# The eighth product with B of a selective scan, formed on GpSimd in ten of sixteen blocks

## The chip, the cores and the metric

The kernel runs on one core of a Trainium2 chip. The metric is device time in microseconds (us). A NeuronCore has five engines that run side by side: TensorE (PE, matrix products), VectorE (DVE), ScalarE (ACT), GpSimd (POOL) and SyncE (SP, here it starts most of the DMAs). Each works through its own queue in order; where one needs another's result, it waits on a semaphore.

## The reference, cut to what matters

Two residual layers of mixer and feed-forward network over `x` (2 x 512 tokens of 512). The change lies in the first mixer, a Mamba block with 1024 channels and 16 states per channel:

```python
def step(state, inp):
    dt_t, B_t, C_t, u_t = inp
    dA = jnp.exp(dt_t[..., None] * A)
    state = state * dA + (dt_t * u_t)[..., None] * B_t[:, None, :]
    y = jnp.einsum('bdn,bn->bd', state, C_t)
    return (state, y)
...
_, ys = jax.lax.scan(step, init, xs)
y = ys.transpose(1, 0, 2) + x * D
y = y * jax.nn.silu(gate)
return y @ W_out.T
```

Behind it come a feed-forward layer with 4-bit weights, an attention over heads within each token, and a second feed-forward layer with experts; each is normalised before and after.

## The kernel before

**Tiling of the scan.** The channels are cut into 8 chunks of 128, one per partition; with two batches that makes 16 blocks (`order`, batch 0 first). A block's 16 states are taken two at a time (`NG = 2`), so a block has 8 steps, and the scan 128. In this text block k is the k-th of the 16 and step g the group of two states within it; step number `s` is 8k + g. Time (512) lies along the free dimension, so that one instruction on 128x1024 elements does two states over all of time.

**What a step does.** On ACT, `exps` (L1002) makes the decay factors `da` = exp(dt A) for the two states, in one of two PSUM buffers that alternate from step to step; it does so for step s + 2, after the scan of step s. On DVE, `times_B` (L1018) forms `bx` = du x B in SBUF, where `du` = dt x u lies in PSUM and holds for the whole block (ACT copies dt there, L1010 in `new_du`; DVE multiplies by u, L1016, at step 0), and `scan` (L1022) runs the recurrence in place, `state = da * state + bx`. On POOL, `times_C` (L1028) multiplies the states by C in place. On PE, `sums` (L1041) adds the two states to the block's `y` in PSUM by products with the identity; the first of a block also adds D x u (L1036). At step 2 of the next block, `fin` (L1047) multiplies `y` by the gate on DVE.

**What sets the order.** The instructions of every engine run in the order in which the program traces them (`pin` ties each to the one before it on its engine, for PE, ACT, DVE and POOL). The main loop (from L1063) writes one pass per step s: the sums of step s - 2 and as much other PE work as a budget of 3.5 us per step allows (`STEP`), then a `tick`, the B product of step s + 1, a second `tick`, the scan of s, the factors of s + 2, the C product of s. A `tick` advances a counter by one and resumes those jobs (generators started by `spawn`) whose time has come; each yields the number of ticks until its next piece. Through them runs everything beside the scan: gates (`silu_of`, three ACT operations L682 to L684 and a product on POOL, L687), the second batch's convolution, the output product of the first batch with its norms (L119, L125, L127, L134, L855, L868), and the first batch's feed-forward layer `ffn0` (PE L947, DVE L935). `pool_turn` keeps such jobs from putting more than one product on POOL in the same step; `pool_at[0]` holds the step whose turn is taken.

**Buffers.** `bx` tiles come from a pool `bxp` of six buffers of 4 KB per partition in turn; one is free again once PE has summed it. `du`, `y` and each `da` have their own place in PSUM. The B and C rows of a batch are spread over all partitions (`states`, L540), one SBUF tile for each step; those of the second batch are loaded by SP during block 7, each after the last use of the tile by the first batch. Behind them on SP's queue come the loads of the output weights `wo` (L862).

**After the scan** PE goes on with what is left of `ffn0`, then the output product of the second batch (L1124), the down product of the first batch's feed-forward layer (L1146), and so on to the end.

Of the kernel before, what the change touches and what calls it, by code (L numbers as in the profile page):

```python
# [9 lines left out]
F32 = mybir.dt.float32  # L10
# [8 lines left out]
P = 128  # L19
B = 2  # L20
S = 512
# [13 lines left out]
NG = 2  # L35
NGI = N_ST // NG
# [20 lines left out]
def tile_sandwich(  # L57
# [5 lines left out]
    nc = tc.nc  # L63

    def pool(scope, name, bufs=1, space=None):
        kw = {"space": space} if space is not None else {"reuse_waits": "tile"}
        return scope.enter_context(tc.tile_pool(name=name, bufs=bufs, **kw))
# [108 lines left out]
    scans, now = [], [0]  # L176
    pool_at = [-9]
# [223 lines left out]
    def pin():  # L401

        seen = nc.cur_bb.bb.instructions
        for ins in seen[behind.get("n", 0) :]:
            if ins.engine not in ORDERED:
                continue
            prev = behind.get(ins.engine)
            if prev is not None:
                tc.add_manual_dep(
                    ins, prev.name,  # L410
                    mybir.DependencyInfo(mybir.DependencyClass.NoSync, mybir.DependencyReason.DATA),
                    reason="order of tracing",
                )
            behind[ins.engine] = ins
        behind["n"] = len(seen)
# [6 lines left out]
    with ExitStack() as mamba:  # L422
# [33 lines left out]
        Bbs = [[None] * NGI for _ in range(B)]  # L456
        Cbs = [[None] * NGI for _ in range(B)]
        st = {}
# [21 lines left out]
        def diag(k):  # L480

            c = k % NCH
            t_ = dgp.tile([P, P], F32, tag="dg", name=f"dg{k}")
            nc.scalar.activation(t_, ident, AF.Copy, scale=ch[:, c, KCONV + 1 : KCONV + 2])
            st["diag", k] = t_
# [49 lines left out]
        def states(b, gi):  # L535

            for lst, lo, nm in ((Bbs[b], 0, "B"), (Cbs[b], R_C - R_B, "C")):
                t_ = bcp.tile([P, NG, S], F32, tag=f"{nm}{gi}", name=f"{nm}{b}_{gi}")
                n0 = lo + gi * NG
                ins = nc.sync.dma_start(  # L540
                    out=t_, in_=scr[b][n0 : n0 + NG, :].partition_broadcast(P)
                )
                lst[gi] = t_
            return ins

        def dt_in(b, c):
            ps = mbank(f"pv{b}_{c}")
            nc.tensor.matmul(ps, wdt[:, ts(c, P)], dtT[b], start=True, stop=True)
            return ps
# [98 lines left out]
            return g1p.tile([P, cols], dt, tag=f"g1{i}", name=name)  # L648

        with ExitStack() as p2:  # L650
            bxp = pool(p2, "bx", 6)
            ps_y = pool(p2, "p2y", 1, PSUM)
            ps_du = pool(p2, "p2du", 1, PSUM)
            ps_da1 = pool(p2, "p2da1", 1, PSUM)
# [13 lines left out]
            def spawn(gen, lag=0):  # L668
                jobs.append([now[0] + lag, gen])

            def tick():
                now[0] += 1
                for job in list(jobs):
                    if job[0] <= now[0]:
                        try:
                            job[0] = now[0] + next(job[1])
                        except StopIteration:
                            jobs.remove(job)
# [13 lines left out]
            def bank_free():  # L692
                return len(turns) < 2 or turns[-2][1] is not None
# [299 lines left out]
            order = [(b, c) for b in range(B) for c in range(NCH)]  # L993
            NS = len(order) * NGI
            bxs = {}

            def exps(s):
                k, gi = divmod(s, NGI)
                b, c = order[k]
                for i in range(NG):  # L1000
                    n = gi * NG + i
                    nc.scalar.activation(  # L1002
                        das[s % 2][:, i, 1:], st["dt", b, c][:, 1:], AF.Exp, scale=A[:, c, n : n + 1]
                    )

            def new_du(k):

                b, c = order[k]
                du = st["du"] = ps_du.tile([P, S], F32, tag="du", name=f"du{b}_{c}")
                nc.scalar.copy(du, st["dt", b, c])  # L1010

            def times_B(s):
                k, gi = divmod(s, NGI)
                b, c = order[k]
                if gi == 0:
                    nc.vector.tensor_mul(st["du"], u[b][c], st["du"])  # L1016
                bx = bxs[s] = bxp.tile([P, NG, S], F32, tag="bx", name=f"bx{b}_{c}_{gi}")
                nc.vector.tensor_mul(bx, st["du"].unsqueeze(1).to_broadcast([P, NG, S]), Bbs[b][gi])  # L1018

            def scan(s):  # L1020
                flat = bxs[s].rearrange("p n t -> p (n t)")
                nc.vector.tensor_tensor_scan(  # L1022
                    flat, das[s % 2].rearrange("p n t -> p (n t)"), flat, 0.0, ALU.mult, ALU.add
                )

            def times_C(s):
                b, c = order[s // NGI]
                nc.gpsimd.tensor_mul(bxs[s], bxs[s], Cbs[b][s % NGI])  # L1028

            def sums(s):  # L1030
                k, gi = divmod(s, NGI)
                b, c = order[k]
                cost = NG * MM
                if gi == 0:
                    y = st["y"] = ps_y.tile([P, S], F32, tag="y", name=f"py{b}_{c}")
                    nc.tensor.matmul(y, st["diag", k], u[b][c], start=True, stop=False)  # L1036
                    cost += MM
                bx = bxs.pop(s)
                for i in range(NG):
                    n = gi * NG + i  # L1040
                    nc.tensor.matmul(st["y"], ident, bx[:, i, :], start=False, stop=(n == N_ST - 1))  # L1041
                return cost

            def fin(k):

                b, c = order[k]
                nc.vector.tensor_mul(g[b][c], g[b][c], st["y"])  # L1047
                st[f"fin{k}"] = now[0]

            def dt_job(k, ps):  # L1050
                dt_out(*order[k], ps)
                release(f"pv{k}")
                yield 1
# [5 lines left out]
            exps(0)  # L1059
            exps(1)  # L1060
            times_B(0)
            free, dt_due = 0.0, None
            for s in range(NS + 3):  # L1063
                k, gi = divmod(s, NGI)
                free = min(free, MM) + STEP
                if gi == 1 and k + 1 < len(order):
                    dt_due = k + 1
                if gi == 2 and k:
                    fin(k - 1)
                for part in ((1, 0) if gi == 2 else (0, 1)):  # L1070
                    if part == 0:
                        if 0 <= s - 2 < NS:
                            free -= sums(s - 2)
                    else:
                        while free > 0 and s < NS:
                            if dt_due and bank_free():
                                turns.append([f"pv{dt_due}", None])
                                spawn(dt_job(dt_due, dt_in(*order[dt_due])), 2)
                                free -= MM
                                dt_due = None  # L1080
                            cost = next(pe, None)
                            if cost is None:
                                break
                            free -= cost
                tick()
                if gi == 4 and k + 1 < len(order):
                    diag(k + 1)
                if 0 < s < NS - 1:
                    times_B(s + 1)
                    if gi == NGI - 2 and k + 1 < len(order):  # L1090
                        new_du(k + 1)
                tick()
                if s < NS:
                    scan(s)
                    if s == 0:
                        times_B(1)
                    if s + 2 < NS:
                        exps(s + 2)
                    times_C(s)
                    if order[k] == (0, NCH - 1):  # L1100
                        states(1, gi)
                pin()
# [6 lines left out]
        with ExitStack() as p3:  # L1109
# [9 lines left out]
            for j in range(NCH // 2):  # L1119
                w = wo_pair(1, 0, j)  # L1120
                for e in range(2):
                    c = 2 * j + e
# [305 lines left out]
```

## Time and profile before

| | us |
|---|---|
| median of 3 runs | 965.91 (965.67 to 966.76) |
| the profiled execution | 963.47 |
| its span, first to last instruction | 961.7 |
| DVE busy over the span | 676.8 |
| PE busy | 869.3 |
| POOL busy | 464.0 |
| ACT busy | 420.7 |
| first scan starts, last scan ends | 74.2, 571.1 |

The profile is of one execution, with every instruction's start and duration. "Busy" is the time in which an engine had an instruction under way; PE's matrix products overlap at their ends, so a busy PE isn't PE at its peak: in the scan's busiest stretches products of 128x512 follow each other every 0.43 us while each is shown as 0.59 us long. Idle time of an engine is put down to the instruction that ended it, shown after an arrow. More than half of the span is the scan, and the kernel's time is the end of the chain that runs through it and the layers behind it.

### The profile page before, as it was taken

Reading aid. Unit: us, or ns where it says so; the run is one execution under the profiler, and the core shown is the slowest. Engines: PE = TensorE matmul, PEld = TensorE weight load, DVE = VectorE, ACT = ScalarE, POOL = GpSimd, SP = SyncE. Lnnn points to the kernel's source line nnn. Section 1 sums busy time; section 2 is a strip of 40 time slices with the busy share of each in tenths; the row PEclk is TensorE's granted clock in tenths of the full one; section 3 lists DMA queues with packets and bytes.
Section 4 is the critical chain, followed back from the end, with each engine's and each line's share of the span. In section 5 each row is a group of like instructions: output and inputs, shape, how many; then the busy total and the mean of one; then the engine's idle time right before and its main releaser. Section 6 shows DMA issues by size and latency. Waiting matters only on the chain.

```text
span 961.7 us, 7188 instructions
## 1 busy us (share of the span) xinstructions
PE 869.3 (90%) x2216; PEld 391.1 (41%) x2216; DVE 676.8 (70%) x783; ACT 420.7 (44%) x631; POOL 464.0 (48%) x335
## 2 busy tenths in 40 slices
PE   6967979878999799769999999998999998999994
PEld 3533433323543344324443434444544444445441
DVE  5959999999999989999989977334510024525225
ACT  4245775656667646565656421124320013412122
POOL 6656796776877757777767664330000000001002
PEclk9988999999999999999999999999999999999998
DMA  6349011100003833300110114336122231100101
GB/s 200 143 159 394 22 37 37 37 29 30 22 26 134 295 128 131 110 0 5 40 44 22 29 40 147 133 127 212 55 62 74 63 100 44 65 12 22 55 0 44
DMA packets 43816, 80.08 MB, mean 83 GB/s; under 512 B 7774, under 2 KB 20937, under 8 KB 43778
## 3 DMA queue, kind: packets, MB, share of 16 engines
q1 hardware_dynamic: 41506, 73.64, 22.6%
q0 software_dynamic: 1984, 5.47, 1.5%
q10 hardware_dynamic: 288, 0.52, 0.1%
q8 instruction: 17, 0.28, 0.1%
q14 instruction: 21, 0.17, 0.1%
HBM read 68.37 MB, written 11.24 MB: 83 GB/s over the span
## 4 chain that ended last, share of the span: by engine, by line
PE 49%; DVE 27%; issue 10%; POOL 5%; DMA 3%; ACT 1%; SPq 0%; DVEq 0%; POOLq 0%; ACTq 0%
DVE bx L1022 10%; PE py L1041 8%; DVE bx L1018 8%; PE pd L1356 6%; PE pup L1293 5%; PE fo L1146 4%; PE fu L367 3%; PE fo L1209 3%; PE fg L367 3%; PE fu L947 3%; POOL bx L1028 3%; PE po L1124 3%; PE fg L947 2%; DMA B<-scr 2%; DVE u L475 2%
## 5 line engine op out<-in xcount | busy, mean ns | idle before, releaser
L1028 POOL TENSOR_TENSOR bx<-bx,C 128x1024 f32<-128x1024 f32 x128 | 302.1, 2360 | 134.3 <-DVE bx L1022 118.1
L1022 DVE TENSOR_TENSOR_SCAN bx<-da,bx 128x1024 f32<-128x1024 f32 x128 | 291.4, 2277 | 0.1
L1041 PE MATMUL py<-bx,ident 128*128 128x512 f32 x512 | 249.0, 617 | 38.3 <-POOL bx L1028 38.2
L1002 ACT ACTIVATE da<-dt,A 128x511 f32<-128x511 f32 x256 | 176.6, 691 | 163.2 <-DVE bx L1022 158.5
L1041 PEld LDWEIGHTS py<-bx,ident 128*128 128x128 f32 x512 | 96.6, 195 | 171.9 <-issue 96.9
L1018 DVE TENSOR_TENSOR bx<-du,B 128x1024 f32<-128x1024 f32 x128 | 154.0, 1204 | 9.5 <-DMA wgu_d<-w_gu 6.2
L1222 DVE TENSOR_TENSOR it<-it,fu 128x512 f32<-128x512 f32 (+1 forms) x11 | 7.6, 687 | 73.9 <-PE fu L367 73.9
L1293 PE MATMUL pup<-hT_l,wup 128*128 128x512 f32 x128 | 57.2, 602 | 0.0
L709 PE MATMUL pg<-xT,w_g 128*128 128x512 f32 x120 | 56.3, 597 | 0.0
L1356 PE MATMUL pd<-wdn,hid 128*128 128x512 f32 x128 | 56.3, 601 | 0.0
L381 POOL TENSOR_TENSOR sd<-ve,half 128x4 f16<-128x4 f16 x2 | 2.1, 1044 | 110.5 <-DVE ve L379 110.5
L127 POOL TENSOR_TENSOR rs_lo<-ve_lo,mhalf 128x1 f32<-128x1 f32 x8 | 5.5, 683 | 78.3 <-DVE ve_lo L125 78.3
L947 PE MATMUL fu<-hT_f,wu 128*128 128x512 f32 (+1 forms) x88 | 41.5, 593 | 0.7 <-ACT dt L553 0.7
L947 PE MATMUL fg<-hT_f,wg 128*128 128x512 f32 (+1 forms) x88 | 41.6, 595 | 0.0
L367 PE MATMUL fg<-hT_f,wg 128*128 128x512 f32 (+1 forms) x88 | 40.2, 593 | 0.7 <-ACT hT_f L171 0.7
L367 PE MATMUL fu<-hT_f,wu 128*128 128x512 f32 (+1 forms) x88 | 40.7, 603 | 0.0
L475 DVE SCALAR_TENSOR_TENSOR u<-px,ch,u 128x511 f32<-128x511 f32 (+2 forms) x48 | 35.8, 746 | 6.1 <-ACT u L468 4.9
L1209 PE MATMUL fo<-wd,it 128*128 128x512 f32 (+1 forms) x88 | 39.8, 595 | 0.0
L1146 PE MATMUL fo<-wd,it 128*128 128x512 f32 (+1 forms) x88 | 38.0, 593 | 0.0
L1356 PEld LDWEIGHTS pd<-wdn,hid 128*128 128x128 f32 x128 | 24.9, 194 | 31.8 <-issue 31.2
L1293 PEld LDWEIGHTS pup<-hT_l,wup 128*128 128x128 f32 x128 | 24.5, 195 | 28.8 <-issue 28.8
L1221 ACT ACTIVATE it<-fg 128x512 f32<-128x512 f32 (+1 forms) x11 | 6.6, 597 | 65.7 <-PE fg L367 65.7
(223 smaller groups left out, 1137.8 us busy)
## 6 DMA issues: line engine op xcount, KB each, us to landing
wo<-in_W_outT SPq DMA_DIRECT2D x20, 512.0 KB
B<-scr SPq DMA_DIRECT2D x16, 512.0 KB
C<-scr SPq DMA_DIRECT2D x16, 512.0 KB
wg<-wgu_d SPq DMA_DIRECT2D x10, 512.0 KB
wu<-wgu_d SPq DMA_DIRECT2D x10, 512.0 KB
w_x<-in_W_in SPq DMA_DIRECT2D x8, 512.0 KB
wgu_d<-w_gu POOLq DMA_DIRECT2D x16, 256.0 KB, 2.3
w_g<-in_W_in SPq DMA_DIRECT2D x8, 512.0 KB
```

The costliest lines, as they stand in the source:

```text
L367: nc.tensor.matmul(ps[:m], w[:, kc, e * P : e * P + m], hT[:, kc, :], start=(kc == 0), stop=(kc == KH - 1),)
L709: nc.tensor.matmul(ps, w[:, k, ts(e, P)], xT[b][:, k, :], start=(k == 0), stop=(k == KH - 1))
L947: nc.tensor.matmul(ps[:m], wt[j][a][:, kc, e * P : e * P + m], hT[:, kc, :], start=(kc == 0), stop=(kc == KH - 1),)
L1002: nc.scalar.activation(das[s % 2][:, i, 1:], st["dt", b, c][:, 1:], AF.Exp, scale=A[:, c, n : n + 1])
L1018: nc.vector.tensor_mul(bx, st["du"].unsqueeze(1).to_broadcast([P, NG, S]), Bbs[b][gi])
L1022: nc.vector.tensor_tensor_scan(flat, das[s % 2].rearrange("p n t -> p (n t)"), flat, 0.0, ALU.mult, ALU.add)
L1028: nc.gpsimd.tensor_mul(bxs[s], bxs[s], Cbs[b][s % NGI])
L1041: nc.tensor.matmul(st["y"], ident, bx[:, i, :], start=False, stop=(n == N_ST - 1))
L1146: nc.tensor.matmul(fo[t], its[i][:m, ts(t, P)], w[:m, e], start=(i == 0), stop=(i == len(IC) - 1),)
L1209: nc.tensor.matmul(fo[t], its[i][:m, ts(t, P)], w[:m], start=(i == 0), stop=(i == len(IC) - 1),)
L1293: nc.tensor.matmul(ps, w[:, kc, ts(e, P)], src[kc], start=(kc == 0), stop=(kc == KH - 1))
L1356: nc.tensor.matmul(pd, hid[kc][:, ts(i, P)], wdn[kc], start=(kc == 0), stop=(kc == INT // P - 1),)
```

## The change

In the blocks with k from 6 to 15 the B product of step 7 is taken from DVE. A job `last_B`, started at step 3 of the block, has ACT copy `du` from PSUM to the second half of a new SBUF tile `bp` (POOL works on it there), and POOL then multiplies that half by the first state's B into the tile's first half, and, two ticks later, by the second state's B in place. `times_B` finds the tile in `bxs` and returns; scan, C product and sums of step 7 use it as they would a `bx` tile. `pool_at[0]` is set for each half, without waiting for a free turn. The pool `bx` has five buffers in place of six, and `bp` one buffer of the same size.

```diff
-            bxp = pool(p2, "bx", 6)
+            bxp = pool(p2, "bx", 5)
@@
                 if gi == 0:
                     nc.vector.tensor_mul(st["du"], u[b][c], st["du"])
+                if s in bxs:
+                    return
                 bx = bxs[s] = bxp.tile([P, NG, S], F32, tag="bx", name=f"bx{b}_{c}_{gi}")
                 nc.vector.tensor_mul(bx, st["du"].unsqueeze(1).to_broadcast([P, NG, S]), Bbs[b][gi])
+
+            def last_B(k):
+
+                b, c = order[k]
+                gi = NGI - 1
+                bx = bxp.tile([P, NG, S], F32, tag="bp", name=f"bp{b}_{c}", bufs=1)
+                nc.scalar.copy(bx[:, NG - 1, :], st["du"])
+                yield 1
+                for i in range(NG):
+                    pool_at[0] = (now[0] - 1) // 2
+                    nc.gpsimd.tensor_mul(bx[:, i, :], bx[:, NG - 1, :], Bbs[b][gi][:, i, :])
+                    yield 2
+                bxs[k * NGI + gi] = bx
@@
+                if gi == 3 and 5 < k < len(order):
+                    spawn(last_B(k))
                 tick()
                 if gi == 4 and k + 1 < len(order):
                     diag(k + 1)
```

In the built program the order of all other instructions on every engine stays as it was: ten B products are gone from DVE, ACT has ten copies more, each right behind the two factors for step 4 (L1002), and POOL twenty products of 128x512 more, ahead of the C products of steps 3 and 4.

## The prediction

> **What bounds the kernel now.** I read the page first: the chain that ended last, then the costliest groups.
>
> ```profile
> PE 49%; DVE 27%; issue 10%; POOL 5%; DMA 3%; ACT 1%; SPq 0%; DVEq 0%; POOLq 0%; ACTq 0%
> ...
> L1028 POOL TENSOR_TENSOR bx<-bx,C 128x1024 f32<-128x1024 f32 x128 | 302.1, 2360 | 134.3 <-DVE bx L1022 118.1
> L1022 DVE TENSOR_TENSOR_SCAN bx<-da,bx 128x1024 f32<-128x1024 f32 x128 | 291.4, 2277 | 0.1
> L1041 PE MATMUL py<-bx,ident 128*128 128x512 f32 x512 | 249.0, 617 | 38.3 <-POOL bx L1028 38.2
> L1002 ACT ACTIVATE da<-dt,A 128x511 f32<-128x511 f32 x256 | 176.6, 691 | 163.2 <-DVE bx L1022 158.5
> ...
> L1018 DVE TENSOR_TENSOR bx<-du,B 128x1024 f32<-128x1024 f32 x128 | 154.0, 1204 | 9.5 <-DMA wgu_d<-w_gu 6.2
> ```
>
> One step of the scan is a B product (1.20) and a scan (2.28) on DVE; ACT then forms the next factors, POOL multiplies by C, PE adds up. I write "block k step g" (k from 0 to 15, g from 0 to 7). The table of stretches, cut at the scans that open blocks 10 to 13 (DVE busy is the third pair, PE the first):
>
> ```profile
> core 0: us, PE busy (x) PEld busy (x) DVE busy (x) ACT busy (x) POOL busy (x), PEclk, DMA share, GB/s
> ...
> 392.20:423.80 31.60, 20.91 (x54) 8.22 (x52) 30.74 (x30) 19.22 (x27) 23.66 (x20) 1.00 0.16 49
> 423.80:452.30 28.50, 26.02 (x59) 11.15 (x60) 28.37 (x20) 18.84 (x28) 20.03 (x10) 0.94 0.00 1
> 452.30:481.40 29.10, 28.41 (x67) 12.24 (x66) 28.97 (x21) 18.32 (x28) 21.90 (x11) 1.00 0.12 36
> ```
>
> DVE is full in nearly every block; PE has room in block 10 and is nearly full in block 12. So the path is DVE's in some blocks and PE's in others (PE without a gap over 1 us from 435.85 to 500). A cut on DVE pays only in the first kind; a delay on DVE costs in both once it exceeds the few us by which DVE leads. The timeline of block 14, steps 2 to 4 (start, us, engine, line):
>
> ```profile
> 520.97 2.28 DVE L1022 TENSOR_TENSOR_SCAN bx<-da,bx 128x1024 f32<-128x1024 f32 x1
> ...
> 523.16 1.20 DVE L1018 TENSOR_TENSOR bx<-du,B 128x1024 f32<-128x1024 f32 x1
> ...
> 523.52 1.42 ACT L1002 ACTIVATE da<-dt,A 128x511 f32<-128x511 f32 x2
> 524.28 2.28 DVE L1022 TENSOR_TENSOR_SCAN bx<-da,bx 128x1024 f32<-128x1024 f32 x1
> ...
> 526.48 1.20 DVE L1018 TENSOR_TENSOR bx<-du,B 128x1024 f32<-128x1024 f32 x1
> 526.59 1.42 ACT L1002 ACTIVATE da<-dt,A 128x511 f32<-128x511 f32 x2 [1.65 <-DVE bx L1022]
> ```
>
> The reader is to see that the product of step 4 (523.16) starts as the scan of step 2 ends (523.25), while ACT's pair of factors for step 4 starts after that scan, because it overwrites what the scan read, and ends 1.7 us later. Today DVE needs nothing from ACT there.
>
> Last, the chain shows where DVE waits for PE anyway (start, us, what), and two price rows, from the instructions of L1010 and L687:
>
> ```profile
> 496.88 0.87 PE fu L947 x2
> ...
> 497.85 0.06 DVE it L935
> ...
> 498.46 2.29 DVE bx L1022
> ```
>
> ```profile
> L1010 ACT COPY du<-dt x16: 567/571/590, 65.4 to 536.6; 128x512 f32<-128x512 f32 x16
> ```
>
> ```profile
> L687 POOL TENSOR_TENSOR it<-ti,it x11: 1263/1269/1707, 445.7 to 593.5; 128x512 f32<-128x512 f32 x10, 96x512 f32<-96x512 f32 x1
> ```
>
> **What the Trainium skill says.** "GPSIMD Engine Reference", section 1 (Specifications), gives POOL no access to PSUM: hence the copy of du, which lies in PSUM. Its section 3.1 has a two-input product about twice as slow as on DVE; the trace agrees (1.27 on POOL, 0.67 for L1016 on DVE, both 128x512). "PSUM — Partial Sum Buffer", section "PSUM bank collisions raise a hardware error": two engines on one bank at once collide, "reads against reads included", and need a semaphore. In the trace of before, ACT writes du and DVE alone reads it, so no run here shows this yet. It decides the case: ACT now reads du in the middle of DVE's reads.
>
> **The change, part by part.**
>
> *Removed.* Ten B products of step 7, 1.20 each. What one is worth is in the last block: its scans of steps 6 and 7, with no product between, start at 566.67 and 568.87, 2.20 apart, where others are 3.31 apart. So 1.11 each, 11.1 in all if DVE were the path everywhere.
>
> *Added on ACT and, by it, on DVE.* The built program's order puts the copy right behind the pair of factors for step 4 in every changed block, and the B product of step 4 now waits for that copy: it reads the same bank. (The copy needs the product of step 3, long done.) Chain from the end of the scan of step 2: 0.03 to ACT, 1.42 for the pair, 0.57 for the copy, 0.03 back: 2.05. Before, the product began 0.08 ahead of that end. So DVE loses 2.13 per block, and everything behind it in DVE's queue, the scan of step 3 first, stands too. Where three silu operations lie ahead of the pair on ACT (blocks 7, 13, 14) the pair started 0.25 later, 2.4. Bounds for the wait: 0 if a copy were done in time, 4 where ACT is busiest; I take 2.13. Net per block: 2.13 - 1.11 = +1.02.
>
> *Added on POOL.* Twice 1.27 per block, ahead of the C products of steps 3 and 4. POOL is free 0.95 in a step of 3.31, but DVE's new wait makes step 3 2.13 longer, so the first half is hidden, even behind a silu product (2 x 1.27 < 0.95 + 2.13); the second delays C of step 4 by 0.3, which the next step absorbs.
>
> *Five buffers and one.* With step 7 in its own buffer, the products of steps 5 and 6 wait for the sums of five steps back, the others six as now. From the starts, this bites once: block 8 step 5 (341.47) needs the sums of block 8 step 0 (from 344.02, its buffer free at about 345.9), late because PE waited for the load of wo. There DVE stands some us longer, but PE's backlog (it begins those sums 5 to 6 us after POOL is done) hides it. The buffer of the eighth product is rewritten five steps after its C product: nothing.
>
> *SP.* The B load for step 7 of the second batch waits for POOL's reading instead of DVE's, earlier than now. The wo load (330.66) stands behind the C load released by block 7's last C product, so it moves with DVE.
>
> **The sum,** walked block by block; lateness against now, DVE / PE at each block's end:
> - 6: ACT has three silu and two pairs ahead of the copy, so the wait is 3.7 (the pair ends at 282.32, the copy at 282.9, the product began at 279.22), but DVE stood 2.24 for the bank of L529 at 285.96: +1.5, less 1.1: 0.4 / 0.4.
> - 7: +1.0: 1.4 / 1.4, the wo load too.
> - 8: the wait falls into the buffer wait; PE saturated: 2.1 / 1.4.
> - 9: at step 4 DVE is 4.2 late, PE's lead there (0.24 to 1) is gone and it stalls: 3.1 / 4.4.
> - 10: wait 2.1 more; the 1.1 of step 7 is lost, since L119 at 417.53 waits for POOL's L855, itself behind a later C product: 5.2 / 5.2.
> - 11 and 12: PE's backlog of 2.0 and 1.5 hides part: 6.2 / 5.6, then 7.3 / 7.2.
> - 13: both effects vanish in the waits for PE at 497.85 (2.49 idle) and 513.13 (0.61): 7.2 / 7.2.
> - 14: wait 2.1 into PE through C of step 3: 8.2 / 9.3.
> - 15: 2.1 more, then 1.1 back, POOL's C products back to back: 9.7 at PE's last sums (573.84).
>
> Behind them PE runs its remaining ffn products without a gap, so 9.7 goes to the end. The profiled execution took 963.47 (span 961.7): 973.2. The median of the runs shown is 965.91, 2.44 above it: 975.6, 1.0% slower.
>
> **Rivals.**
> 1. The wait is hidden, faster: if the copy were done before the scan of step 2 ends, the 2.13 vanish and 1.11 counts in the DVE-led blocks (6, 7, 9, 10, 14, 15): -6.7, 959.2. For it: ACT idles 158.5 us for DVE in all. Against: that idle is just the wait for the scan that releases the pair ahead of the copy. It decides only if the copy ends under 1.0 after that scan. 7%.
> 2. POOL takes the gain: no wait, but in blocks 14 and 15 a silu product (1.27) and the first half (1.27) stand before C of step 3, for which PE waits within 0.06, and block 10's L855 slips; near zero, 966. 4%.
> 3. The stalls cost more: after PE's 3.02 idle at 425.31 four matmuls took 3.53, not 1.88 to 1.98. If blocks 9, 10, 14 and 15 get such stalls, 4 x 1.1 to 1.7, about +5 on the sum: 980.5. 11%.
>
> The likeliest, the sum above: 78%; its own range 971 to 980, from +0.5 to +1.4 per block. To hold eight in ten with the others: 969 to 981. Slower by over 0.2% (some 2 us, what a measurement tells from no change): 0.90; within: 0.03; faster: 0.07.
>
> **What would show it.** In the changed profile: DVE idle about 2.1 before the B product of step 4, ended by ACT's copy, ten times, some 20 us in all; scans of steps 5 and 6 2.2 apart; the last sums near 583.5; POOL busy 25 more. I am wrong if no idle time on DVE names the copy, or if DVE's idle is there and the end moved by under 4 (PE's backlog hid more) or over 14.

## The result and the profile after

| | before | after |
|---|---|---|
| median of the runs taken together, us | 965.79 (6 runs) | 971.85 (6 runs) |
| ratio, with its 95% interval | | 1.0059 (1.0042 to 1.0075) |
| the profiled execution, us | 963.47 | 972.27 |
| its span, us | 961.7 | 970.5 |

The change makes the kernel 6.1 us slower by these medians, 5.7 by the ratio. The forecast was 975.6, with a range of 969 to 981: the direction holds, and the time lies 3.8 below the middle. The two profiled executions differ by 8.8, more than the medians do; 2.0 of this arises in block 2, ahead of the first changed block, and is taken up in the last section. So the changed part of the scan costs 6.8 in the profiles. In `after` the B product is L1020, ACT's copy L1027, POOL's halves L1031, the scan L1037, the C product L1043 and the sums L1056.

The page of after: the chain's shares by engine, and the costliest groups (after the bar: busy us, mean ns of one; then idle us before them and what ended most of it).

```profile
PE 48%; DVE 24%; issue 9%; ACT 7%; POOL 4%; DMA 2%; DVEq 0%; SPq 0%; POOLq 0%; ACTq 0%
...
L1043 POOL TENSOR_TENSOR bx<-bx,C 128x1024 f32<-128x1024 f32 x118 | 277.8, 2357 | 110.2 <-DVE bx L1037 98.7
L1037 DVE TENSOR_TENSOR_SCAN bx<-da,bx 128x1024 f32<-128x1024 f32 x118 | 268.0, 2278 | 0.1
L1056 PE MATMUL py<-bx,ident 128*128 128x512 f32 x472 | 231.5, 621 | 39.5 <-POOL bx L1043 39.5
L1002 ACT ACTIVATE da<-dt,A 128x511 f32<-128x511 f32 x256 | 176.6, 691 | 170.6 <-DVE bx L1037 149.6
L1020 DVE TENSOR_TENSOR bx<-du,B 128x1024 f32<-128x1024 f32 x118 | 142.6, 1209 | 28.7 <-ACT bp L1027 22.9
```

The reader is to see two things. ACT's share of the chain was 1% and is 7%: the path now runs through ACT. And the B product, which stood idle 9.5 us in all, mostly for DMAs, stands 28.7, of which 22.9 ends with a copy of 0.58 us. The instructions of L1027, and who waits for them:

```profile
L1027 ACT COPY bp<-du x10: 577/577/579, 284.3 to 562.6; 128x512 f32<-128x512 f32 x10
...
who waited for it (us, times):
  DVE bx L1020: 22.9, 10
```

Ten copies, ten waits, 2.3 each on the mean. One of them from near, block 9 in the timelines of DVE and then ACT of after (start, us, engine, line; in brackets the idle time before and its releaser):

```profile
369.63 2.28 DVE L1037 TENSOR_TENSOR_SCAN bx<-da,bx 128x1024 f32<-128x1024 f32 x1
373.91 1.23 DVE L1020 TENSOR_TENSOR bx<-du,B 128x1024 f32<-128x1024 f32 x1 [2.00 <-ACT bp L1027]
```

```profile
371.95 1.41 ACT L1002 ACTIVATE da<-dt,A 128x511 f32<-128x511 f32 x2
373.30 0.58 ACT L1027 COPY bp<-du 128x512 f32<-128x512 f32 x1
```

The same place in DVE's timeline of before:

```profile
367.81 2.28 DVE L1022 TENSOR_TENSOR_SCAN bx<-da,bx 128x1024 f32<-128x1024 f32 x1
370.00 1.20 DVE L1018 TENSOR_TENSOR bx<-du,B 128x1024 f32<-128x1024 f32 x1
```

Before, the product starts 2.19 after the scan's start, that is as the scan ends; after, 4.28. In between lie ACT's pair of factors, which needs the end of that scan, and the copy that is queued behind the pair.

**What moved besides.** The text ahead of the prediction says that the order of all other instructions stays as it was on every engine. For SP's queue that is not so: a few loads trade places in it, and the first load of the output weights `wo`, which stood behind the last C load, is issued 13 us earlier. SP's timeline of before, then of after:

```profile
330.25 0.32 SPq L540 DMA_DIRECT2D C<-scr  x1
330.66 13.06 SPq L862 DMA_DIRECT2D wo<-in_W_outT  x6
```

```profile
317.44 0.38 SPq L862 DMA_DIRECT2D wo<-in_W_outT  x1
...
334.49 9.88 SPq L862 DMA_DIRECT2D wo<-in_W_outT  x5
```

And what PE makes of it at the end of block 7, before and then after:

```profile
336.24 7.08 PE L916 MATMUL po<-wo,g 128*128 128x512 f32 x12 [2.92 <-DMA wo<-in_W_outT]
```

```profile
337.07 1.98 PE L916 MATMUL po<-wo,g 128*128 128x512 f32 x4
340.27 3.70 PE L916 MATMUL po<-wo,g 128*128 128x512 f32 x8 [1.22 <-DMA wo<-in_W_outT]
```

Before, PE waits 2.92 for the first `wo`, and the twelve products then take 7.08; after, it begins at once and waits 1.22 for the second `wo`. PE's lateness against before, 3.8 at the end of block 7, is 0.7 in block 8 (each with the 2.0 of block 2).

### The profile page after: what moved, and what is told of

Its sections match the earlier page's. It is cut to its first block, busy times and chain, and to the rows that moved or that the text cites. A ratio compares the mean times of both kernels' runs of the same rounds, so it can differ in the third digit from the quotient of the medians.

```text
span 970.5 us, 7173 instructions
## 1 busy us (share of the span) xinstructions
PE 875.3 (90%) x2216; PEld 391.0 (40%) x2216; DVE 666.3 (69%) x773; ACT 425.5 (44%) x641; POOL 487.4 (50%) x355
## 4 chain that ended last, share of the span: by engine, by line
PE 48%; DVE 24%; issue 9%; ACT 7%; POOL 4%; DMA 2%; DVEq 0%; SPq 0%; POOLq 0%; ACTq 0%
DVE bx L1037 10%; PE py L1056 8%; PE pd L1373 6%; DVE bx L1020 6%; PE pup L1310 5%; PE fo L1163 4%; PE fu L367 3%; PE fo L1226 3%; PE fg L367 3%; POOL bx L1043 3%; PE po L1141 3%; ACT da L1002 3%; PE pg L709 2%; PE fu L947 2%; DVE u L475 1%
## 5 line engine op out<-in xcount | busy, mean ns | idle before, releaser
L1043 POOL TENSOR_TENSOR bx<-bx,C 128x1024 f32<-128x1024 f32 x118 | 277.8, 2357 | 110.2 <-DVE bx L1037 98.7
L1037 DVE TENSOR_TENSOR_SCAN bx<-da,bx 128x1024 f32<-128x1024 f32 x118 | 268.0, 2278 | 0.1
L1056 PE MATMUL py<-bx,ident 128*128 128x512 f32 x472 | 231.5, 621 | 39.5 <-POOL bx L1043 39.5
L1002 ACT ACTIVATE da<-dt,A 128x511 f32<-128x511 f32 x256 | 176.6, 691 | 170.6 <-DVE bx L1037 149.6
L1020 DVE TENSOR_TENSOR bx<-du,B 128x1024 f32<-128x1024 f32 x118 | 142.6, 1209 | 28.7 <-ACT bp L1027 22.9
L1056 PEld LDWEIGHTS py<-bx,ident 128*128 128x128 f32 x472 | 88.3, 195 | 166.8 <-issue 87.0
```

The source lines that it names most:

```text
L1002: nc.scalar.activation(das[s % 2][:, i, 1:], st["dt", b, c][:, 1:], AF.Exp, scale=A[:, c, n : n + 1])
L1037: nc.vector.tensor_tensor_scan(flat, das[s % 2].rearrange("p n t -> p (n t)"), flat, 0.0, ALU.mult, ALU.add)
```

## The experiments

Theory: the ten waits for the copy make the loss; the removed products give part of it back; the moved `wo` load takes off some 3 us more. Rivals: that POOL's added work or the missing sixth buffer costs the time; that the load's move means nothing. Every ratio is to the kernel before, in runs on the same chip; behind it stands its 95% interval, and a difference in us beside it is the ratio times the time of before.

### The wait: the copy ahead of the pair, and the copy alone

In the first kernel the copy is traced at step 2 of the block, so that it stands ahead of ACT's pair of factors for step 4; all else is the change (the `wo` load stays behind the C loads here):

```diff
+            def copy_du(k):
+                b, c = order[k]
+                bx = st["bp"] = bxp.tile([P, NG, S], F32, tag="bp", name=f"bp{b}_{c}", bufs=1)
+                nc.scalar.copy(bx[:, NG - 1, :], st["du"])
...
-                bx = bxp.tile([P, NG, S], F32, tag="bp", name=f"bp{b}_{c}", bufs=1)
-                nc.scalar.copy(bx[:, NG - 1, :], st["du"])
+                bx = st["bp"]
...
                     times_B(s + 1)
+                    if gi == 2 and 5 < k < len(order):
+                        copy_du(k)
```

> The change with ACT's copy of du moved ahead of the pair of factors for step 4, so that it runs during the scan of step 2; the load of wo stands behind the C loads as before the change. If DVE's new wait for that copy is the cause of the loss, DVE no longer idles before the B product of step 4 (22.9 us in the changed kernel, here under 2), and the time falls to 0 to 7 us under the kernel before (nearer 0 if POOL's two extra products now delay the C product of step 3). If POOL's twenty products are the cause, it stays 5 us or more above it.

Measured: 965.04 (14 runs), ratio 1.0008 (0.9995 to 1.0022), +0.8. All the loss is gone with the place of one instruction on ACT. The fairest comparison is with the third kernel below (1.0095), where the `wo` load stands behind too and the copy stays in its place: 8.4 us between the two. The copies, and who waits for them:

```profile
  DVE bx L1020: 2.3, 3
```

POOL does the same work here as in after, and there are five buffers: so neither is what was lost and came back. But the ten removed products then gain nothing either. PE at the end of block 7, then DVE in block 8:

```profile
337.81 7.48 PE L916 MATMUL po<-wo,g 128*128 128x512 f32 x12 [4.82 <-DMA wo<-in_W_outT]
```

```profile
347.95 1.23 DVE L1020 TENSOR_TENSOR bx<-du,B 128x1024 f32<-128x1024 f32 x1 [6.88 <-issue]
```

DVE comes earlier to block 8 and stands there, where PE is late because of `wo`. The view names no instruction that ended this wait; that it is for a free buffer is read from the kernel with five buffers and no other edit, further down, which has the same wait in the same place. The later runs take this up.

In the second kernel the copy stays where the change has it, and nothing uses it: POOL's halves and the use of the tile are taken out of `last_B`, and DVE makes all the products.

> Only the copy is added, in the place where the change has it; DVE forms all eight products and POOL none of them (the copied tile is read by nobody). If the wait for the copy is the cause, DVE idles 20 us or more before the B product of step 4, and the time is 9 to 14 us above the kernel before: more than the change's 6, because no product is saved. If POOL's products are the cause, within 2 us of the kernel before.

Measured: 983.64 (5 runs), ratio 1.0193 (1.0172 to 1.0214): +18.6, above the range expected. The wait is as in after, 21.2 of it put down to the copy, in nine of the ten blocks:

```profile
L1020 DVE TENSOR_TENSOR bx<-du,B 128x1024 f32<-128x1024 f32 x128 | 154.2, 1206 | 29.8 <-ACT bp L1026 21.2
```

So the wait does it without any work on POOL. Against after, which has the first `wo` load early as this one has, the ten products add 12.9 us here, with an uncertainty of some 2.6. That is no less than the 11.1 of which DVE is freed: with the wait in place DVE is late in nearly every block, and what it is freed of counts in full or nearly so.

### The moved load: held back, and moved alone

The third kernel is the change with the first `wo` load tied behind the last C load of the second batch, as in the kernel before:

```diff
+                if (b, i, j) == (0, 0, 0):
+                    with tc.issue_after(st["C7"].ins):
+                        nc.sync.dma_start(out=w, in_=w_out[j])
+                    return w
...
-                        states(1, gi)
+                        st["C7"] = states(1, gi)
```

> The change with the first load of wo held behind the last C load on SP's queue, where the kernel before has it; in the changed kernel it had moved ahead of eleven DMAs. If that move is why the change cost 3 us less than the sum said, this is about 3 us slower than the changed kernel (9 above the kernel before), and PE begins the po products of block 8 some 3 us later. If not, equal to the changed kernel, 6 above.

Measured: 973.19 (4 runs), ratio 1.0095 (1.0081 to 1.0109): +9.2. With the order of SP on which the forecast was built, the cost is what the forecast summed up (9.7). With the difference that was there before block 6 taken off, the sums of block 8 begin 2.2 later than before here, and 1.3 earlier than before in after. PE's timeline at the end of block 7:

```profile
337.03 8.41 PE L920 MATMUL po<-wo,g 128*128 128x512 f32 x12 [3.65 <-DMA wo<-in_W_outT]
```

The fourth kernel is the kernel before with the first two `wo` loads issued in mid-block; the order on the other engines is untouched:

```diff
                 ex = w4(expert_w, "wex", LAT // P, LAT)
+                st["wo"] = {0: wo_pair(0, 0, 0)}
...
                     spawn(out(), 2)
+                st["wo"][1] = wo_pair(0, 0, 1)
...
-                ws = {}
+                ws = st["wo"]
```

> The kernel before with nothing but the first two loads of the out-projection's weights issued earlier on SP's queue (after C_3 and after C_5 of the second half of the scan). In the changed kernel's trace the first of these loads had moved ahead by 13 us without the change asking for it. Theory A, that this moved load is what made the changed kernel some 3 us cheaper than the forecast's sum: PE's wait of 2.92 us ahead of the out-projection in block 7 goes, and with it the half-speed matmuls behind it; the kernel is 2 to 4 us faster than before. Rival B, that something later is the limit (PE's queue is busy anyway, and the wait only moves): within 1 us of before.

Measured: 962.52 (22 runs), ratio 0.9974 (0.9963 to 0.9985): 2.5 us faster. PE at the same place, where neither a wait nor slow products are left in the output product:

```profile
336.96 5.42 PE L918 MATMUL po<-wo,g 128*128 128x512 f32 x12
```

(The four sums just ahead of it took 3.56 in this profile and 1.98 in that of before, so the gain read from it alone would be uncertain.) It holds both ways: the load's place is worth some 3 us to the changed kernel (9.2 against 6.1 by its medians or 5.7 by its ratio; the intervals leave it open by 2) and 2.5 to the one before.

### Five buffers

The kernel before with `pool(p2, "bx", 5)` and nothing else:

> The kernel before with five buffers for bx in place of six, nothing else. If the sixth buffer mattered, slower by 2 us or more, with DVE idle before B products. By the prediction's reading it bites once, in block 8, under PE's backlog: within 1 us of the kernel before.

Measured: 967.88 (15 runs), ratio 1.0029 (1.0015 to 1.0044), +2.8: missed. DVE in block 8, here and then before:

```profile
347.51 1.22 DVE L1018 TENSOR_TENSOR bx<-du,B 128x1024 f32<-128x1024 f32 x1 [4.39 <-issue]
```

```profile
345.99 1.23 DVE L1018 TENSOR_TENSOR bx<-du,B 128x1024 f32<-128x1024 f32 x1 [1.13 <-issue]
```

The wait is where the prediction put it, at the product of step 5; before, the product of step 6 had a smaller one. DVE is 4.5 later at once and 1.4 later at the end of the block, and PE takes over this 1.4 in block 9. In this profile PE loses 1.7 more at the turn to block 11: after the same 3.02 of idle time as before, its four sums took 3.78 in place of 3.53, and the two pairs of products next to them 2.07 each in place of 1.12. Whether the buffer has to do with that isn't shown.

With the early loads the sums of block 8 come sooner, so the buffer should matter less. The same edit on top of them:

> The kernel before with the early loads and with five state buffers instead of six: the base for what the ten products are worth in the one with both (0.9956 of before). The early loads with six buffers gave 0.9974. Theory A, that the fifth buffer is missed in block 8 whatever the loads do (it cost 0.0029 with the loads as in the kernel before): 0.9985 to 1.001, so the ten products are worth 3 to 5 us of the 11.1 us that DVE is freed of. Rival B, that the buffer only hurt because the out-projection was late: 0.9965 to 0.998, and the ten products are worth 1 to 2 us.

Measured: 962.99 (22 runs), ratio 0.9984 (0.9971 to 0.9998), between the two theories: about 1 us for the buffer, with intervals that overlap those of 0.9974. This is the base for what the products are worth.

### What the ten products are worth

With the wait and the late load out of the way: the early copy and the early loads together.

> The change with ACT's copy of du moved ahead of its pair of factors, and with the first two loads of the out-projection's weights issued early. The copy alone gave +0.0008 in ratio, with 2 us of lateness in block 8, where that load landed late. Theory A, that the wait for the copy and the late load are the two things that hide the gain of the ten removed products: 3 to 7 us faster than before. Rival B, that with five state buffers the scan waits in block 8 anyway and POOL's halves hold up the C products in blocks 13 to 15: within 2 us of before.

Measured: 960.31 (6 runs), ratio 0.9956 (0.9938 to 0.9973), 4.2 us faster than before. From the base of 0.9984, whose interval just overlaps this one, the ten products give 2.7 us of the 11.1 of which DVE is freed. Where does the rest go? First, to POOL's place ahead of the C products? POOL's halves one step later (`if gi == 4` at the `spawn`, and the tile entered in `bxs` at once):

> As the one with both, but POOL makes its two halves one step later, behind the C product of step 3 instead of ahead of it. Theory A, that POOL's halves delay the C product of step 3 and through it PE's sums in blocks 13 to 15: another 1 to 2.5 us faster than the one with both. Rival B, that they only trade places with the C products of steps 4 and 5, or that the scan of step 7 then waits for the second half: same as the one with both within 1 us, or slower.

Measured: 960.73 (6 runs), ratio 0.995 (0.9931 to 0.997): the same, within the intervals: POOL's place is not it. Second, does it depend on the block? The eighth product on POOL in blocks 6 and 7 alone (`5 < k < 8`), in blocks 8 to 15 alone (`7 < k`), and the latter with the halves one step later:

> As the one with both (early copy, early loads, five state buffers), but POOL makes the eighth product only in blocks 6 and 7 instead of in all ten. Theory A, that from block 8 on PE's own queue is the limit (its lateness stays within about 1 us from there on in the one with both, while DVE loses each 1.1 us that it gains before the next block is over): the eight products of blocks 8 to 15 are worth nothing, and the time is that of the one with both within 1.5 us (ratio 0.994 to 0.997). Rival B, that the later eight products carry most of what the change gains: 2 to 6 us slower than the one with both, that is 0.998 of before or above.

> The complement: early copy, early loads, five state buffers, and POOL makes the eighth product in blocks 8 to 15 alone. Theory A (PE is the limit from block 8 on): no gain over the kernel with the early loads alone, 0.9974 of before, and some 1 us more where the fifth buffer is missed in block 8: 0.997 to 1.0. Rival B (each removed product counts): 6 to 8 us under the kernel with the early loads alone, 0.990 or below.

> Early copy, early loads, five state buffers; POOL makes the eighth product in blocks 8 to 15 alone, and its halves one step later. With the halves ahead of the C product of step 3 this gave 0.9963. Theory A, that the products of blocks 6 and 7 gain nothing and that the place of the halves is worth under 1 us: 0.994 to 0.997. Rival B, that the halves ahead of step 3's C product cost about a microsecond in each of several late blocks: 0.993 or below.

Measured: 963.33, 0.999 (0.9975 to 1.0005); 960.87, 0.9963 (0.9949 to 0.9978); and 960.53, 0.9973 (0.9949 to 0.9998). The two products alone are worth nothing over the base of 0.9984; the eight, 1 to 2 us of 8.9, with intervals that overlap the base's. The theory that only the two early ones count fell, and so did the one that each counts in full. The trace shows what becomes of the two. PE at the end of block 7, in the kernel with both:

```profile
331.75 3.70 PE L918 MATMUL po<-wo,g 128*128 128x512 f32 x8
338.11 3.12 PE L918 MATMUL po<-wo,g 128*128 128x512 f32 x4 [2.66 <-DMA wo<-in_W_outT]
```

DVE and PE come earlier to the output product, and PE now waits for the third `wo`, which was still queued last; behind it DVE stands 4.56 at the product of step 5 of block 8 (6.10 in the kernel with two blocks alone). So one load more is moved ahead:

```diff
                 st["wo"][1] = wo_pair(0, 0, 1)
+                st["wo"][2] = wo_pair(0, 0, 2)
```

> As the one with both, with the third load of the out-projection's weights issued right behind the second one as well; no other queue's order changes. In the one with both, PE waits 2.66 us for that third load in block 7 (2.99 in the one with two products alone), where it doesn't wait in the kernel with the early loads and all products on DVE: DVE is 1 to 2 us earlier there, the load is not. Theory A, that the gain of the products of blocks 6 and 7 is eaten by this third load: PE's wait goes, and the kernel is 1 to 3 us faster than the one with both: 0.9925 to 0.9945 of before. Rival B, that the DMA engines are full there (366 GB/s on the mean from 326 to 341 us), so that the load only delays those of B and C behind it: same as the one with both, 0.995 to 0.997, or slower.

Measured: 958.52 (6 runs), ratio 0.9936 (0.9914 to 0.9957), 6.2 us faster than before: the lowest median of all, though its interval overlaps that of the kernel with both. PE there:

```profile
330.57 5.42 PE L919 MATMUL po<-wo,g 128*128 128x512 f32 x12
```

The wait is gone, DVE's in block 8 too, and in its profile PE is 7.3 earlier than before in block 8. From the base, in which PE doesn't wait for the third load, the ten products are now worth 4.6 us (0.9984 to 0.9936). In this profile the rest is lost behind block 8. From the last scan of block 8 to the last of block 15 DVE makes seven products less than before, yet takes 212.7 us (before 211.6): its idle time in that stretch is 15.3, before 6.8. It waits 2.66 for POOL's L855 in block 10 (0.44 before), 0.61 and 1.50 for ACT's copy in blocks 11 and 12, where even the early copy isn't done in time, and 2.31, 1.65, 2.55 and 2.56 for PE's `fu` from block 13 on (2.49, 0.61, 1.33 and 1.32 before). PE's lead is 5.1 at the last sums. That is the other part of the answer, as one profile shows it: late in the scan what DVE is freed of turns into waits for PE, POOL and ACT.

## Why the prediction was right in direction and 3.8 us too high

**The wait: right.** The forecast: a wait of DVE at the product of step 4, ended by ACT's copy, ten times, some 20 us in all. Measured: ten, 22.9 us. The length of 2.05 behind the end of the scan is 1.95 to 2.00 in blocks 8, 9, 10, 11 and 15, 3.80 in block 6 (3.7 forecast), 2.48, 2.23 and 2.23 in blocks 7, 13 and 14 (2.4 forecast) and 2.23 in block 12. The first run shows that it is the cause: with 2.3 of it left the loss is gone. That the two readers of `du` take turns agrees with what the Trainium skill says in "PSUM — Partial Sum Buffer", section "PSUM bank collisions raise a hardware error" (the words that the prediction quotes, "reads against reads included", stand on that page under "Terms"); what the runs add is that the wait is priced by what stands ahead of the other reader in its queue, not by its own 0.58 us.

**The removed products: right as part of the sum.** Where no product lies between, two scans follow back to back in 4.46 us, and each removed product gives DVE 1.1 back; with the wait in place they count in full or nearly so (12.9 us for the ten between the second run and after, more than 11.1 but not beyond the noise).

**POOL: right.** It is 23.4 us busier (25 forecast), and later halves change nothing that the intervals could tell.

**The sum, block by block.** In the kernel with the load held back the end comes 9.2 later by the ratio and 9.6 in the profile's last sums, for 9.7. PE's lateness there (the start of the last sums of a block, less that of before) after blocks 7, 8, 10, 12, 14 and 15 is 0.1, 2.1, 5.2, 7.3, 9.2 and 9.6; the forecast had 1.4, 1.4, 5.2, 7.2, 9.3 and 9.7. So block 7's entry was 1.3 too high, and from block 8 on the walk holds within 0.7. In after the last sums start at 582.75, 8.9 later than before, where the forecast had 583.5; but this agreement is partly luck, since block 2's 2.0 us and the load's gain cancel in part.

**The step that failed: the one on SP.** "The wo load (330.66) stands behind the C load released by block 7's last C product, so it moves with DVE", and from it the entry for block 7, "the wo load too". SP's queue isn't tied to the order of the program as the other four are; in after the first load stands ahead, and the prediction took its place from the kernel before. The entry thus kept PE's wait of 2.92 and the slow products behind it, later by what DVE is late; in after they are 1.22 and none. The mis-set term is worth some -3 us, most of the gap between the sum (9.7) and the medians (6.1).

**A smaller one: "PE's backlog hides it" of the fifth buffer.** It does not: the buffer alone costs 2.8 with the loads as they were, and 1.4 of it can be followed in the trace from DVE to PE. In the sum this is not seen, because the change's own wait stands in the same block and the two overlap.

**The rivals.** The first, a hidden wait, had 959.2 (-6.7), and no run of the change is like that. Made by hand, with the copy ahead, it gave +0.8: the `wo` load and the buffer ate what DVE gained. Only with the three loads ahead does the run come to -6.2. That this is near the rival's value is partly luck: 2.5 of it the loads give to the kernel before as well, and in that profile DVE gains nothing from the products of blocks 9 to 15, on four of which the rival counted. The second, that POOL takes the gain, had the value of the run with the copy ahead (near zero), but not its cause: there DVE's long wait is the one in block 8. One part of it is seen, L855 in block 10, for which DVE waits 2.67 in that run, before 0.44; with POOL's halves later it is 2.68. The third, that PE runs slowly after stalls, isn't needed in blocks 9 to 15.

## What to carry to other kernels

Before work is moved to an engine that needs a copy, ask who else reads the copy's source and what stands ahead of the copy in its own queue: here 0.58 us of copy held another engine for 2.0 to 3.8, because a pair of instructions that waited for that engine stood ahead of it, and tracing the copy one step sooner left 2.3 of the 22.9 us. Compare the built order of every queue, the DMA queue too: a load that changes place without being touched was worth about half of the change's whole effect. And when an engine is freed of work and the end doesn't move, look at the first wait by which another one stops: with three loads issued earlier a gain of nothing became one of 6 us, of which the loads by themselves give some 2.5.

## What the runs showed of the hardware that was not expected

The same wait is followed by fast or slow matrix products. PE's timeline with the halves later, and with two blocks alone:

```profile
336.28 1.98 PE L918 MATMUL po<-wo,g 128*128 128x512 f32 x4 [2.99 <-DMA wo<-in_W_outT]
```

```profile
339.76 3.78 PE L918 MATMUL po<-wo,g 128*128 128x512 f32 x4 [2.99 <-DMA wo<-in_W_outT]
```

Both waited 2.99; four products then took 1.98 in one and 3.78 in the other, at a granted clock of 1.00 and of 0.50. So the length of the idle time alone doesn't decide when PE falls to about half speed, and the runs don't show what does. The same happens in block 2, where the kernels don't differ. The stretch around it in before and in after (the last three columns: granted clock of PE, DMA share, GB/s):

```profile
136.00:150.00 14.00, 12.60 (x27) 5.30 (x28) 13.93 (x12) 9.02 (x13) 10.25 (x7) 0.88 0.03 13
```

```profile
136.00:150.00 14.00, 13.20 (x22) 5.21 (x23) 11.82 (x9) 7.78 (x10) 9.97 (x7) 0.63 0.03 13
```

The clock is 0.88 in one execution and 0.63 in the other, and DVE stands 2.18 us more in the second, waiting for ACT's `u`, which waits for PE. Of the fourteen profiles of this text, five (after and four others, among them the kernel before with five buffers) lose 2.3 us in block 2 against before, and the others nothing, though no edit touches that block. So two profiles can differ by this much ahead of any change, which is a reason to read a difference of a few us from medians and the place from the profile.
